# Attention's projections made for all batches in its first steps, experts dealt evenly over the steps, and the last batch divided on the chip

## The chip, the cores and the metric

The kernel runs on one core of one Trainium2 chip. The metric is the device time of the whole program in microseconds (us). The chip's engines are TensorE (PE in the profile; PEld is its weight load), VectorE (DVE), ScalarE (ACT), GpSimd (POOL) and SyncE (SP), which here only issues transfers. Each engine takes its instructions in order.

## What is computed

Eight batches of 512 tokens of width 256 pass through two layers, all in float32. Layer 0 is a state-space mixer and a mixture of experts; it is not changed here except for one small call. Layer 1, in the reference's own words cut short:

```python
xn = _layernorm(x)
q = x @ Wq;  latent_kv = (x @ Wk + x @ Wv) @ W_down_kv        # 256 -> 64
k_rec = latent_kv @ W_up_k;  v_rec = latent_kv @ W_up_v       # 64 -> 256
scores = clip(einsum('bhqd,bhkd->bhqk', qh, kh) * scale) * decay
out = softmax(clip(scores)) @ vh                               # 16 heads of 16
x = x + out @ Wo + ffn(xn)
```

The `ffn` sends each token to its two likeliest of eight experts; the eighth does nothing, and the other seven take at most 512 tokens each: `relu(in @ W1) @ W2`, scaled by the router's share and added to the token's row.

## The kernel before

**Layer 0** and the norm of layer 1 come first (up to about 1101 us). A generator `late` (line 576) makes the normed rows, keeps their transpose in HBM (`xtd1`), and makes batch 0's projections by calling `project`.

**The attention stage** starts at line 1281 with pools of its own; its schedule is written by hand from line 1486. There are 128 steps, `n` = 0 to 127: for each batch `b` (16 steps), each group `g` of four heads, each block `c` of 128 queries. In program order, round `n` of the loop issues:

- step n's scores (lines 1411 to 1422): four matmuls into `s_ps`, then on VectorE a clip, a multiplication by the decay band with a row maximum, and a negation;
- step n-1's four exponentials on ScalarE (line 1426);
- step n-2's transposes into `p_ps` (line 1433), four of 128 columns per head, and ScalarE's copies to `pT` (line 1434);
- in even rounds the product with v for two finished steps (`o_ps`, line 1442). I call a step even or odd by whether its round has that product.

Between these lie *slots*: calls of `fill` (line 1505), four a round up to round 63, then four in even rounds and three in odd ones. A slot takes one *piece* of other work, the first there is: the piece half done, then the list `urgent`, then `idle`. A piece is what a generator does up to its next `yield`. The other work:

- **Projections** (`project`, line 236, called through `inputs_of`, line 1294). For each batch: the latent (`lp`, 2 chains' worth of matmuls over 512 columns, copied to `lat` as 64 x 512), q (`qp`), k (`kp`), v (`vp`, four times 288 columns, with a row of ones in `lat` that makes the column of ones for the softmax sums). That is nine pieces. q and k pass through one buffer `qkc`, are stored in HBM (`qd`, `kd`) and loaded again by 32 transfers of 16 rows each that put each head on a 32-partition strip (`spread`, line 1274; six are issued each round by `load_some`). The pieces for batch b+1 enter `urgent` at round 16b + 6; its transposed input `xT` is asked at round 16b + 3.
- **Routing, sends, experts.** `follow` (line 1522) runs once a round: the rest of `late` in rounds 0 to 2, routing, then two `sends` a round (each scatters a tile of 128 rows to two slots by indirect transfers of GpSimd, line 1315, and has VectorE scale the tile into `x_sb`, line 1322). When these end, the round is called `ready` (25 here), and three rounds later `experts` (line 1221) enters `idle`. An expert's half is 17 pieces: one of transposes (`e_tp`), eight of the first layer (`e_hp`), eight of the second (`e_yp`, a quarter of a chain each). Fourteen halves are 238 pieces. Results are added to `x1` in HBM by GpSimd (line 1267).
- **Division and output.** After a group's last block `divide` (line 1448) copies `o_ps` to `os`, stores it in HBM (`od`), and for each pair of groups loads the heads back packed (`oT`, line 1466) and the sums by themselves (`sm`, line 1467), takes the reciprocals, sends them through HBM to be spread over partitions (`rb`), and multiplies (line 1478). Each of these steps is one round apart. Then `finish` (line 1371), four pieces in `urgent`, multiplies by Wo (`fin`) and adds into `x_sb`.
- **Combine** (line 1388): when no piece is left, `more` makes GpSimd add the eight batches of `x1` into `x_sb` by transfers (line 1391) and send out finished batches (line 1386); later batches go out as they finish.
- **The last batch's last two groups** are divided on the chip (`Ending`, line 1337): transpose, divide, transpose back, project, store. Groups 0 and 1 go through `divide` as in other batches.

`bank` is one PSUM buffer for all pieces of the stage, so that a piece's matmuls wait for the copy of the piece before.

Of the kernel before, what the change touches and what calls it, by code (L numbers as in the profile page):

```python
# [9 lines left out]
FP = mybir.dt.float32  # L10
# [7 lines left out]
P = 128  # L18
# [41 lines left out]
def tile_kernel(ctx: ExitStack, tc: tile.TileContext, t, out: bass.AP):  # L60
# [175 lines left out]
    def project(xT, lat, flat, vt, rows, bank, spread=None):  # L236


        lp = bank("lp", [DL, S])
        for k in range(KC):  # L240
            T.matmul(lp, w_kv[:, k, :], xT[:, k, :], start=(k == 0), stop=(k == KC - 1))  # L241
        A.copy(lat[:DL, :], lp)
        yield
        for n in ("q", "k"):
            fl = flat(n)
            for o in range(KC):
                ps = bank(n + "p", [P, S])
                if n == "q":
                    for k in range(KC):
                        T.matmul(  # L250
                            ps, w_q[:, k, o * P : (o + 1) * P], xT[:, k, :], start=(k == 0), stop=(k == KC - 1)
                        )
                    A.mul(fl[:, o, :], ps, 1.0 / 16.0)
                else:
                    T.matmul(ps, w_uk[:, o * P : (o + 1) * P], lat[:DL, :], start=True, stop=True)
                    A.copy(fl[:, o, :], ps)
                yield
            Y.dma_start(out=rows[n].rearrange("(o p) s -> p o s", p=P), in_=fl)
            if spread:
                spread(n)  # L260
        for c in range(TPB):
            vp = bank("vp", [P, VW])
            T.matmul(vp, lat[:, c * P : (c + 1) * P], w_uv, start=True, stop=True)  # L263
            A.copy(vt[:, c, :], vp)
            yield

    def rows_qk():
        return {n: dram.tile([DM, S], FP, name=n + "d", tag=n + "d", bufs=2) for n in ("q", "k")}
# [221 lines left out]
    with ExitStack() as es:  # L490
# [85 lines left out]
        def late():  # L576
# [19 lines left out]
            for b in range(B):  # L596
# [55 lines left out]
                if b == 0:  # L652
                    lat = tl.tile([DL + 1, S], FP, name="lat", tag="lat")
                    G.memset(lat[DL : DL + 1, :], 1.0)
                    yield from project(
                        xT, lat, lambda n: tl.tile([P, KC, S], FP, name=n + "c", tag="xn"), vt0, qk0,
                        lambda name, shape: bank(name, shape, "e"),
                    )

        def second_weights():  # L660

            nonlocal l1c, tl, w_r, rb, w_q, w_o, w_uk, w_uv, w_kv, band, slot1, iota_n, proj1, vt0, qk0
            es.close()
            l1c = ctx.enter_context(tc.tile_pool(name="l1c", bufs=1, side="right"))
            tl = tls.enter_context(tc.tile_pool(name="tl", bufs=1, side="right"))
            w_r = load("w_r", [P, KC, NE], l1c)
            rb = load("rb", [P, NE], l1c)
            w_q = load("w_q", [P, KC, DM], l1c)
            w_o = load("w_o", [P, KC, DM], l1c)
            w_uk = load("w_uk", [DL, DM], l1c)  # L670

            w_uv = ctile("w_uv", [DL + 1, VW], pool=l1c)
            G.memset(w_uv, 0.0)
            hv = w_uv[:, : AH * (AD + 1)].rearrange("p (h e) -> p h e", e=AD + 1)
            Y.dma_start(out=hv[:DL, :, :AD], in_=t["w_uv"])
            G.memset(hv[DL : DL + 1, :, AD : AD + 1], 1.0)
            slot1 = ctile("slot1", [P, NTILE, 2], I32, l1c)
            iota_n = ctile("iota_n", [P, NTILE], pool=l1c)
            G.iota(iota_n, pattern=[[P, NTILE]], base=-NT, channel_multiplier=1, allow_small_or_imprecise_dtypes=True)
            proj1 = ctile("proj1", [P, NTILE, NE], pool=l1c)  # L680
            vt0 = ctile("vt0", [P, TPB, VW], pool=l1c)
            qk0 = rows_qk()

            band = ctile("band", [P, NBAND], pool=l1c)
            G.iota(
                band, pattern=[[1, NBAND]], base=P - S, channel_multiplier=-1, allow_small_or_imprecise_dtypes=True
            )

            w_kv = ctile("w_kv", [P, KC, DL], pool=l1c)
            both = tl.tile([P, 2, KC, DM], FP, name="w_kt", tag="xr", bufs=2)  # L690
            Y.dma_start(out=both[:, 0], in_=t["w_kt"])
            Y.dma_start(out=both[:, 1], in_=t["w_vt"])
            w_dn = ctile("w_dn", [P, KC, DL], pool=tl)
            Y.dma_start(out=w_dn, in_=t["w_dn"])
            yield
            A.activation(band, band, AF.Abs)
            A.activation(band, band, AF.Exp, scale=-DECAY)
            V.tensor_tensor(both[:, 0], both[:, 0], both[:, 1], ALU.add)
            yield
            wp = bank("wp", [P, KC, DL], "e")  # L700
            for k in range(KC):
                for o in range(KC):
                    T.matmul(
                        wp[:, k, :], both[:, 0, o, k * P : (k + 1) * P], w_dn[:, o, :],
                        start=(o == 0), stop=(o == KC - 1),
                    )
            V.tensor_copy(w_kv, wp)
            yield
# [439 lines left out]
    with tc.tile_pool(name="a1", bufs=1) as p1, tc.tile_pool(name="a2", bufs=2) as p2, tc.tile_pool(  # L1148
# [125 lines left out]
        def spread(rows, got, n, by=None):  # L1274

            for g in range(4):
                wide = p2.tile([P, S], FP, name=n + "T", tag=n + "T", bufs=6)
                for i in range(4):
                    h = 4 * g + i
                    to, of = wide[32 * i : 32 * i + AD, :], rows[n][h * AD : (h + 1) * AD, :]  # L1280
# [4 lines left out]
                got[n].append(wide)  # L1285
# [8 lines left out]
        def inputs_of(b, xT, got):  # L1294
            rows = rows_qk()
            got["v"] = p2.tile([P, TPB, VW], FP, name="vt", tag="vt")
            yield from project(
                xT, lat, lambda n: p1.tile([P, KC, S], FP, name=n + "c", tag="qkc"), got["v"], rows, bank,
                lambda n: spread(rows, got, n),
            )  # L1300
# [26 lines left out]
        def ask_rows(b):  # L1327
            to_send[b] = r1b.tile([P, TPB, DW], FP, name="xs", tag="xs", bufs=B)
            Y.dma_start(out=to_send[b][:, :, :DM], in_=rows_of(xn1, b))
# [6 lines left out]

        class Ending:
# [3 lines left out]
            def __init__(self, b, c, op, held):  # L1341
                self.i, self.c, self.op, (self.oT, self.os) = b * TPB + c, c, op, held
# [6 lines left out]
            def divide(self):  # L1349
# [3 lines left out]
                tq = tq.rearrange("p g (i r) -> p (g i) r", r=32)  # L1353
                sm = p2.tile([P, 8], FP, name="smq", tag="smq")
                V.reciprocal(sm, tq[:, :, AD])
                self.oq = p2.tile([P, 8, AD], FP, name="oq", tag="oq")
                V.tensor_tensor(self.oq, tq[:, :, :AD], bc(sm, 2, [P, 8, AD]), ALU.mult)

            def back(self):
                tp = psum.tile([P, P], FP, name="tb", tag="s_ps", bufs=4)  # L1360
                T.transpose(tp, self.oq.rearrange("p h d -> p (h d)"), ident)
# [9 lines left out]
        def finish(b, oT):  # L1371
# [10 lines left out]
            if b in combined:  # L1382
                send(b)

        def send(b):
            G.dma_start(out=rows_of(out, b), in_=x_sb[:, b * TPB : (b + 1) * TPB, :])

        def combine():

            for b in range(B):  # L1390
                G.dma_start(out=x_sb[:, b * TPB : (b + 1) * TPB, :], in_=rows_of(x1, b), accum_op=ALU.add)
                combined.add(b)
            yield
            for b in finished:
                send(b)
# [52 lines left out]
        def divide(b, g, op, od, rd, held):  # L1448


            os = p1.tile([P, S], FP, name="os", tag="row", bufs=2)
            A.copy(os, op)
            if b == B - 1 and g == 2:
                held.append(os)
                return
# [27 lines left out]
        lat = p1.tile([DL + 1, S], FP, name="lat", tag="lat")  # L1483
        G.memset(lat[DL : DL + 1, :], 1.0)

        with tc.manual_schedule(engines=ENGINES):
            got = {"q": [], "k": [], "v": vt0}
            spread(qk0, got, "q", Y)
            spread(qk0, got, "k", A)
            finished, combined = set(), set()  # L1490
            urgent, idle, chains = [], [], []
# [3 lines left out]
            half_done = []  # L1495
            late_left = True
# [8 lines left out]
            def fill():  # L1505

                while queue := half_done or urgent or idle:
                    try:
                        if next(queue[0]):
# [8 lines left out]
            def more():  # L1518
                if ready is not None and n > ready + 3:
                    next(rows, None)  # L1520
# [23 lines left out]
            inputs = {0: got}  # L1544
            for n in range(N + 3):

                if n < N:
                    b, g, c = steps[n]
                    if (g, c) == (0, 3) and b + 1 < B:
                        xT = p2.tile([P, KC, S], FP, name="xT", tag="xT")  # L1550
                        Y.dma_start(out=xT, in_=xtd1[b + 1])
                    if (g, c) == (1, 2) and b + 1 < B:
                        inputs[b + 1] = {"q": [], "k": []}
                        urgent.append(inputs_of(b + 1, xT, inputs[b + 1]))
                    if (g, c) == (0, 0):
                        od = dram.tile([4, 4, 32, S], FP, name="od", tag="od", bufs=2)
                        rd = dram.tile([AH, S], FP, name="rd", tag="rd", bufs=2)
                        scratch = (od, rd, [])
                    now = Step(b, g, c, inputs[b])
# [3 lines left out]
                load_some(6)  # L1563
                if n == N + 1:
# [66 lines left out]
def layout(i):  # L1631
# [9 lines left out]
    def every(v):  # L1641
# [32 lines left out]
        "w_uv": i["L1_attn_W_up_v"].reshape(DL, AH, AD),  # L1674
# [28 lines left out]
```

## Time and profile before

| | |
|---|---|
| median of 3 runs | 2100.85 us (2100.71 to 2111.31) |
| the profiled execution | 2100.49 us; its span 2098.8 us, mean granted TensorE clock 0.933 |
| busy in the span | TensorE 1857.0 (88%), VectorE 1433.7 (68%), ScalarE 1178.8 (56%), GpSimd 629.1 (30%) |
| attention's first scores, first clip | 1103.98, 1106.09 us |
| first and last expert result sent (L1267) | 1366.9, 1975.3 us |
| mean of one exponential (L1426), one copy to pT (L1434), one clip (L1416) | 726, 590, 683 ns |

In the profile's groups a row gives line, engine, operation, output and inputs, shape and count; then busy time in us and the mean of one in ns; then the engine's idle time just before these instructions and what ended it. Busy times of neighbouring TensorE groups overlap, since matmuls are pipelined. A window's row gives its length, each engine's busy time and instruction count, the granted TensorE clock, the share of the DMA engines and the rate in GB/s.

### The profile page before, as it was taken

What the parts mean: (1) busy time and instruction counts of PE and PEld (TensorE: products, weight loads), DVE (VectorE), ACT (ScalarE), POOL (GpSimd) and SP (SyncE); (2) the same over time, 40 slices, a digit from 0 to 9 for tenths busy, and PEclk for the clock granted to TensorE, in tenths of its full rate; (3) what the DMA queues carried; (4) which work ended last, traced back from release to release, by engine and by line L of the source; (5) the groups of instructions that cost most, each with busy time, mean ns of one, the idle gap of its engine ahead of it and who ended that gap; (6) DMA issues with size and microseconds to landing.
All of it is one profiled execution on the core that took longest, in us unless ns stands there. A gap on an engine that the chain in (4) does not pass through costs nothing. (4 is left out here: it accounts for less than half of the span.)

```text
span 2098.8 us, 33158 instructions
## 1 busy us (share of the span) xinstructions
PE 1857.0 (88%) x11684; PEld 1227.0 (58%) x11684; DVE 1433.7 (68%) x3305; ACT 1178.8 (56%) x2548; POOL 629.1 (30%) x572
## 2 busy tenths in 40 slices
PE   5666999999999999977767877999999999999987
PEld 5333676677677677744544444566656666565544
DVE  5684757666575766678648976766666677777786
ACT  2243454535454454545425565767777777777776
POOL 0048645445464544445420154010000100000300
PEclk9877999999999999998876879899999999999989
DMA  7113654656564555444432232222312222221440
GB/s 260 61 51 113 224 192 161 202 175 201 166 205 152 195 184 174 140 145 133 148 100 96 80 115 69 78 82 64 88 53 83 67 85 85 64 89 52 74 129 27
DMA packets 150063, 255.03 MB, mean 122 GB/s; under 512 B 23457, under 2 KB 108116, under 8 KB 137992
## 3 DMA queue, kind: packets, MB, share of 16 engines
q1 hardware_dynamic: 111912, 132.31, 19.9%
q0 software_dynamic: 28512, 110.92, 17.0%
q10 hardware_dynamic: 9472, 9.67, 1.4%
q8 instruction: 93, 1.52, 0.3%
q14 instruction: 74, 0.61, 0.1%
HBM read 184.74 MB, written 73.09 MB: 123 GB/s over the span
## 5 line engine op out<-in xcount | busy, mean ns | idle before, releaser
L1416 DVE TENSOR_SCALAR s<-s_ps 128x512 f32<-128x512 f32 x512 | 317.7, 683 | 235.9 <-PE s_ps L1411 182.5
L1426 ACT ACTIVATE s<-s,ng 128x512 f32<-128x512 f32 x512 | 354.1, 726 | 24.1 <-DVE ng L1422 20.8
L1433 PE MATMUL p_ps<-ident,s 128*128 128x128 f32 x2048 | 296.8, 289 | 57.8 <-ACT pT L1434 49.8
L1433 PEld LDWEIGHTS p_ps<-ident,s 128*128 128x128 f32 x2048 | 245.3, 148 | 141.5 <-ACT pT L1434 84.8
L1418 DVE CUSTOM_DVE_ANT_0 s<-s,band 128x512 f32<-128x512 f32 x512 | 322.9, 687 | 0.0
L1434 ACT COPY pT<-p_ps 128x512 f32<-128x512 f32 x512 | 278.0, 590 | 72.1 <-PE p_ps L1433 57.1
L1267 POOL DMA_INDIRECT x<-e_yo,e_to x28 | 44.1, 1576 | 606.0 <-ACT e_yo L1266 541.0
L732 PE MATMUL pj<-xT,w_in 128*128 128x512 f32 x384 | 203.2, 656 | 16.6 <-DVE cv L745 13.7
L1411 PE MATMUL s_ps<-kT,qT 16*128 16x512 f32 x1024 | 167.3, 685 | 19.1 <-DVE s L1416 12.4
L544 PEld LDWEIGHTS h_ps<-xdT,w 128*128 128x128 f32 x1248 | 149.2, 192 | 22.4 <-issue 21.6
L544 PE MATMUL h_ps<-xdT,w 128*128 128x128 f32 x1248 | 152.8, 276 | 3.0 <-DMA w<-in_w_dram,w_idx 3.0
L745 DVE SCALAR_TENSOR_TENSOR cv<-pj,w_conv_w,cv 128x511 f32<-128x511 f32 (+2 forms) x192 | 143.1, 746 | 11.1 <-ACT cv L741 7.1
L562 PE MATMUL y_ps<-w,hT 128*128 128x256 f32 x624 | 148.9, 383 | 0.0
L908 POOL TENSOR_TENSOR au<-da,half 128x512 f32<-128x512 f32 x64 | 78.9, 1233 | 224.8 <-PE seg L924 122.7
L1442 PE MATMUL o_ps<-pT,vt 128*32 128x256 f32 x2048 | 139.4, 414 | 0.0
L562 PEld LDWEIGHTS y_ps<-w,hT 128*128 128x128 f32 x624 | 117.2, 193 | 32.5 <-issue 17.9
L732 PEld LDWEIGHTS pj<-xT,w_in 128*128 128x128 f32 x384 | 71.7, 205 | 100.0 <-issue 91.3
L982 POOL TENSOR_TENSOR yT<-yT,ex 128x512 f32<-128x512 f32 (+1 forms) x48 | 59.6, 1243 | 222.8 <-DVE ex L981 164.0
L1248 PE MATMUL e_hp<-e_xdT,e_w 128*128 128x256 f32 x448 | 121.7, 394 | 3.1 <-ACT e_xdT L1233 2.3
L1261 PE MATMUL e_yp<-e_w,e_hT 128*128 128x256 f32 x448 | 120.0, 390 | 0.2
L937 ACT ACTIVATE mt<-seg,mid 64x64 f32<-64x64 f32 x512 | 109.5, 309 | 0.8
L1442 PEld LDWEIGHTS o_ps<-pT,vt 128*32 128x32 f32 x2048 | 64.4, 117 | 77.9 <-issue 48.0
(292 smaller groups left out, 3019.6 us busy)
## 6 DMA issues: line engine op xcount, KB each, us to landing
ex<-exd SPq DMA_DIRECT2D x96, 128.0 KB
u<-in_u_dram SPq DMA_DIRECT2D x16, 512.0 KB
xtd<-xT SPq DMA_DIRECT2D x16, 512.0 KB
fr<-fdd SPq DMA_DIRECT2D x64, 128.0 KB
xT<-xtd SPq DMA_DIRECT2D x15, 512.0 KB
od<-os SPq DMA_DIRECT2D x30, 256.0 KB
e_w<-in_ei_dram SPq DMA_DIRECT2D x7, 1024.0 KB
e_w<-in_eo_dram SPq DMA_DIRECT2D x7, 1024.0 KB
```

What stands on the lines that cost most here:

```text
L544: T.matmul(hp[:, i, :], w1[:, k * FF + f * P : k * FF + (f + 1) * P], xdT[:, k * P : (k + 1) * P], start=(k == 0), stop=(k == KC - 1),)
L562: T.matmul(yp, hT[f // 4][:, f % 4, :], w2[:, f * DM : (f + 1) * DM], start=(f == 0), stop=(f == FC - 1))
L732: T.matmul(pj, w_in[:, k, o * P : (o + 1) * P], self.xT[:, k, :], start=(k == 0), stop=(k == KC - 1))
L745: V.scalar_tensor_tensor(cv[:, s:], pj[:, : S - s], conv_w[:, q, 3 - s : 4 - s], cv[:, s:], ALU.mult, ALU.add)
L1248: T.matmul(hp, w1[:, k, f * P : (f + 1) * P], xdT[:, k, :], start=(k == 0), stop=(k == KC - 1))
L1411: T.matmul(sp[i], self.q[r, cols], self.k[r, :], start=True, stop=True)
L1416: V.tensor_scalar(self.p[i], sp[i], -CLAMP, CLAMP, ALU.max, ALU.min)
L1418: V.tensor_tensor_reduce(out=self.p[i], in0=self.p[i], in1=band[:, at : at + S], scale=1.0, scalar=-3.0e38, op0=ALU.mult, op1=ALU.max, acc ...
L1426: A.activation(self.p[i], self.p[i], AF.Exp, bias=self.ng[:, i : i + 1])
L1433: T.transpose(pp[:, k, :], self.p[i][:, k * P : (k + 1) * P], ident)
L1434: A.copy(pT[i][:, :, cc * P : (cc + 1) * P], pp)
L1442: T.matmul(op[32 * i : 32 * i + 32, half * 2 * P : (half + 1) * 2 * P], self.v[:, k, h * (AD + 1) : h * (AD + 1) + 32], pT[i][:, k, :], st ...
```

## The change

1. `project` now lays the latent out in two halves: tokens 0 to 255 on partitions 0 to 63, 256 to 511 on 64 to 127. `lp` is four matmul calls of 256 columns instead of two of 512, and its copy is 128 x 256. k and v are made for each half from its own 64 partitions, with the up-projection weights present in both halves. v is made without the column of ones, in two copies instead of four; the ones are set once in the buffer. Seven pieces instead of nine.
2. `inputs`, a new generator, makes the projections of batches 1 to 7 one after the other, through two `qkc` buffers, stores q, k and v in HBM with room for all batches, and asks `xT` one batch ahead (for the first and the last batch at the batch's own start). Two of its pieces may be taken in each round once `late` has ended (`early`), before expert pieces and after urgent ones. `inputs_of(b + 1)`, at round 16b + 8, only loads v and lists the 32 loads of q and k.
3. Expert pieces are taken only while `spent < due()`: 238 pieces in equal shares over the rounds from `ready + 3` to 117.
4. The combine starts when all 238 are spent: batches 7 and 0 to 5 are added, batch 6 once it is finished, and then batches 0 to 6 are sent out together.
5. Batch 7's groups 0 and 1 are divided on the chip too (`first_heads`, eight pieces in `urgent`), each group copied to a buffer `ol`.
6. Four buffers instead of eight for the rows to be sent (`xs`). In layer 0's part two idle yields follow batch 0's projection, which has two pieces fewer.

```diff
+        lp = bank("lp", [P, HS])
         for k in range(KC):
-            T.matmul(lp, w_kv[:, k, :], xT[:, k, :], start=(k == 0), stop=(k == KC - 1))
-        A.copy(lat[:DL, :], lp)
+            for i, r in SIDES:
+                T.matmul(
+                    lp[r, :], w_kv[:, k, :], xT[:, k, i * HS : (i + 1) * HS], start=(k == 0), stop=(k == KC - 1)
+                )
+        A.copy(lat, lp)
...
+        for i, r in SIDES:
+            ps = bank("kp", [P, KC, HS])
             for o in range(KC):
+                T.matmul(ps[:, o, :], w_uk[r, o * P : (o + 1) * P], lat[r, :], start=True, stop=True)
+            A.copy(fl[:, :, i * HS : (i + 1) * HS], ps)
+            yield
...
+        for i, r in SIDES:
+            vp = bank("vp", [P, 2, AH * AD])
+            for c in range(2):
+                T.matmul(vp[:, c, :], lat[r, c * P : (c + 1) * P], w_uv[r, :], start=True, stop=True)
+            A.copy(
+                vt[:, 2 * i : 2 * i + 2, : AH * (AD + 1)].rearrange("p t (h e) -> p t h e", e=AD + 1)[:, :, :, :AD],
+                vp.rearrange("p t (h e) -> p t h e", e=AD),
+            )
+            yield
...
+        def inputs():
+
+            xT = {}
+
+            def ask_xT(b):
+                if b < B:
+                    xT[b] = p2.tile([P, KC, S], FP, name="xT", tag="xT")
+                    Y.dma_start(out=xT[b], in_=xtd1[b])
+
+            ask_xT(1)
+            for b in range(1, B):
+                if b + 1 < B - 1:
+                    ask_xT(b + 1)
+                elif b == B - 1:
+                    ask_xT(b)
+                    yield
+                rows = rows_qk()
+                yield from project(
+                    xT.pop(b), lat, lambda n: p1.tile([P, KC, S], FP, name=n + "c", tag="qkc", bufs=2), vt1, rows, bank
+                )
+                vd = dram.tile([P, TPB, VW], FP, name="vd", tag="vd", bufs=B)
+                Y.dma_start(out=vd, in_=vt1)
+                kept[b] = (rows, vd)
...
+        def first_heads(oT, os):
+
+            for c in range(TPB):
+                at = slice(c * P, (c + 1) * P)
+                tq = bank("tq", [P, 2, P])
+                for k in range(2):
+                    T.transpose(tq[:, k, :], os[k][:, at], ident)
+                oq = columns(tq)
+                yield
+                tp = bank("tb", [P, P])
+                T.transpose(tp, oq, ident)
+                A.copy(oT[:, 0, at], tp)
+                yield
...
+            for b in (B - 1, *range(B - 2)):
+                add(b)
+            yield
+            while B - 2 not in finished:
+                yield
+            add(B - 2)
+            for b in range(B - 1):
+                G.dma_start(out=rows_of(out, b), in_=x_sb[:, b * TPB : (b + 1) * TPB, :])
...
+            WORK = NE1 * 2 * (1 + FC + 2 * FC // 2)
+            LAST = 117
+            spent = 0
+
+            def due():
+
+                return WORK * (n - ready - 2) / (LAST - ready - 2)
...
-                while queue := half_done or urgent or idle:
+                nonlocal spent, early
+                while queue := half_done or urgent or (early and ahead) or (idle if idle and spent < due() else []):
                     try:
+                        early -= queue is ahead
+                        spent += queue[0] is work
...
             def more():
-                if ready is not None and n > ready + 3:
+                if spent == WORK:
                     next(rows, None)
...
                 load_some(6)
+                early = 0 if late_left else 2
```

## The prediction

> **What bounds the kernel now.** I read the slices first, then the chain that ended last, then windows of the trace cut where the attention stage changes character, then the groups and waits inside those windows.
>
> ```profile
> PE   5666999999999999977767877999999999999987
> ...
> PEclk9877999999999999998876879899999999999989
> ...
> PE 34%; ACT 7%; DVE 4%; DMA 2%; issue 2%; another core or an unknown queue 0%; ACTq 0%; DVEq 0%; SPq 0%
> ```
>
> A slice is 52.5 us. The change lives in the attention stage, slices 22 to 40 (from 1101 us). TensorE fills slices 26 to 38, and the chain is mostly TensorE. In slices 22 to 25 TensorE is not full (7, 8, 7, 7) and its clock is 0.6 to 0.9; the last two slices are not full either.
>
> ```profile
> core 0: us, PE busy (x) PEld busy (x) DVE busy (x) ACT busy (x) POOL busy (x), PEclk, DMA share, GB/s
> ...
> 1131.00:1181.00 50.00, 45.20 (x299) 26.71 (x297) 43.88 (x121) 36.74 (x67) 0.16 (x1) 0.87 0.22 75
> 1181.00:1337.00 156.00, 123.37 (x792) 68.06 (x796) 115.23 (x346) 91.17 (x163) 62.77 (x64) 0.78 0.28 89
> 1337.00:1664.00 327.00, 312.32 (x2250) 206.50 (x2243) 221.03 (x585) 236.27 (x452) 22.77 (x15) 1.00 0.25 71
> 1664.00:1978.00 314.00, 303.25 (x2226) 197.51 (x2225) 226.33 (x594) 235.87 (x453) 21.36 (x14) 0.99 0.26 74
> 1978.00:2021.00 43.00, 34.58 (x272) 19.12 (x274) 35.52 (x93) 32.37 (x58) 15.01 (x14) 0.89 0.88 193
> 2021.00:2099.00 78.00, 63.15 (x532) 38.96 (x524) 56.75 (x150) 56.52 (x107) 0.75 (x1) 0.95 0.09 29
> ```
>
> I place the 128 steps by each step's first clip (L1416). **Early**, steps 3 to 27 (1131 to 1337): routing and sends, loose, cold clock. **Middle**, steps 28 to 110 (1337 to 1978): experts, TensorE 96% busy. Steps 111 to 117 (1978 to 2021): experts gone, VectorE sets the pace, about 5.05 us an undisturbed step. **Tail**, 118 to the end: 78 us.
>
> ```profile
> L1433 PE MATMUL p_ps<-ident,s 128*128 128x128 f32 x1440 | 195.1, 277 | 23.4 <-ACT pT L1434 23.4
> L1248 PE MATMUL e_hp<-e_xdT,e_w 128*128 128x256 f32 x448 | 121.7, 394 | 3.1 <-ACT e_xdT L1233 2.3
> L1261 PE MATMUL e_yp<-e_w,e_hT 128*128 128x256 f32 x448 | 120.0, 390 | 0.2
> L1411 PE MATMUL s_ps<-kT,qT 16*128 16x512 f32 x720 | 106.3, 648 | 2.0 <-DVE s L1416 2.0
> L1442 PE MATMUL o_ps<-pT,vt 128*32 128x256 f32 x1432 | 88.9, 389 | 0.0
> L1375 PE MATMUL fin<-w_w_o,oT 128*128 128x256 f32 x80 | 22.7, 408 | 4.9 <-ACT kc L256 4.6
> L250 PE MATMUL qp<-xT,w_w_q 128*128 128x512 f32 x40 | 19.6, 613 | 0.0
> L263 PE MATMUL vp<-w_uv,lat 65*128 65x288 f32 x40 | 13.7, 424 | 0.0
> L255 PE MATMUL kp<-lat,w_w_uk 64*128 64x512 f32 x20 | 11.2, 641 | 0.0
> L241 PE MATMUL lp<-xT,w_kv 128*64 128x512 f32 x20 | 9.7, 605 | 0.0
> ```
>
> ScalarE's groups of the same window have this row:
>
> ```profile
> L256 ACT COPY kc<-kp 128x512 f32<-128x512 f32 x10 | 5.9, 586 | 11.9 <-PE kp L255 6.6 <-DMA qd<-qc 5.2
> ```
>
> The first fence has TensorE's groups of 1337 to 2021, 90 steps. A step's own TensorE work is (195.1 + 106.3 + 88.9) / 90 = 4.33 us. Five batches' projections, qp + vp + kp + lp, add 54.2 us, 10.84 each; five finishes 22.7. The L256 row shows the single projection buffer at work: k's copy waited 5.2 us for q's store. And after 1980:
>
> ```profile
> DVE sm L1472 <- DMA sm<-od: 4.1, 1, 4.1
> ```
>
> VectorE, the pace setter there, stands 4.1 us behind the tiny load of batch 6's sums, at 2015.7, just after the combine's burst (DMA share 0.88 in that window).
>
> **Part by part: the projections leave the middle.** Groups overlap: with e_tp's 8.8 us they sum to 717.7, against 650.1 us of busy TensorE (the three windows' sum). So 54.2 us is 54.2 x 0.906 = 49 of busy time; at 96% busy, 51 us. Steps 37 to 41, with a projection and a finish, took 42.4 us; their other work (5 x 4.33, seven expert pieces at 0.86, four finish pieces at 1.13) explains 32, leaving 10. The two agree: **-51 us**. The q-store wait goes too; it lies inside these 51, as SPq's loads do.
>
> **Experts dealt evenly.** 238 pieces over steps 28 to 117 are 2.64 a step. Steps 64 to 69 hold neither projection nor finish: 44.0 us and 21 pieces, so a piece costs (44.0 - 6 x 4.33) / 21 = 0.86 us. Steps 111 to 117 give 43 - 7 x 4.33 = 13 us of TensorE slack. A dealt step then needs 4.33 + 2.64 x 0.86 = 6.6 us, above VectorE's 5.05 (5.7 with its divisions) and ScalarE's 5.4 (504.5 busy in that window, less the projections' 23, over 90): TensorE sets it. **-13 us**. In the other direction, odd steps (no values) with three pieces waited 0.43 us for ScalarE (6.31 us, 5.88 busy), so I give back **+2**, with bounds 0 and +25 (0.3 us a step). Together 684 becomes 622.
>
> **Seven projections in steps 3 to 28.** 50 pieces at two a step; four slots exist before step 64, urgent work first, so they fit, and batch 1 is complete (8 calls, steps 3 to 6) before step 8 asks for it. Per batch: lp was two chains of 512 columns, 1.93 us; two column halves may run side by side, as the four 32-wide strips of L1442 do (32 matmuls in 1.93 us in the timeline), so 0.97 to 1.93. [...] The old lp, kp and vp rows already had 64 columns or 64 rows, and their price of 10 us was measured in place[...]. [...] by the L1442 row it halves. I take 0.97; the difference, 7 us in all, goes into the range. kp and vp: 16 matmuls of 256 columns at finish's 1.13 us per four are 4.5, qp 3.9. Sum 9.4, x 0.906 = 8.5 us; seven are 60, and 20 were there: **+40 us of TensorE work at full clock**.
>
> How much shows? At full clock the early work is 25 x 4.33 + 20 + 4.5 + 1.3 = 134 us of its 206. After the change 174. What stays: seven TensorE gaps of 2 us and more during the sends, 23 us (the largest have ScalarE waiting on an unknown queue); 3 us for batch 1's xT, now asked in the very piece that reads it (a 512 KB transfer took 2.8), with scores and transposes queued behind it on TensorE; about 12 for cold windows after stalls; 4% ordinary idle, 7; 3 where routing holds VectorE. Total 222, **+16 us**. Two readings bound it. [...] The row says 0.78 in the sends, but 1131 to 1181, with a projection inside, 0.87. If the clock stays at 0.78, 40 / 0.78 = 51 us shows in full: early 257. If the work only fills idle time: 206, or 200 with a warmer base. I take 222 because the 0.87 row, denser, is the nearer.
>
> **Side costs.** SPq: the stores of q and k and the xT loads move among the sends' xs loads and the first divisions' loads; a store waits for ScalarE's copy, a us or so, and what queues behind it is asked steps ahead. The store and reload of v are 14 more issues at about 0.4 us, over 100 steps. All k and q loads start at a batch's step 8 with six a step; done by 14. I cost all this at nothing; without that slack a late kT would cost its 2 to 3 us. xs with four buffers: a load waits for scatters issued two steps, some 15 us, earlier: 0, at most a few us on SPq. Weights and memsets of v before 1101: 0, bounds -3 to +3. ScalarE: v in two copies instead of four: inside the sum.
>
> **Last batch and combine.** Batch 7's groups 0 and 1: four times two transposes, a reciprocal (0.20) and a multiply (0.29), a transpose, a 0.27 copy: about 2.0 us of VectorE, against 0.35 x 2 + 0.69 x 2 before: +1, where VectorE sets the pace. No loads of sums behind the burst: the 4.1 us was batch 6's and goes because the burst now starts after step 117; it is inside the 13. The burst (some 27 us from 1979.5) moves into steps 118 to 126, where nothing loads. ScalarE's 3 us disturbances move with it: +3. The expert generator's end raises the counter past its target, so what remains of the write-back is issued after the loop; GpSimd has nothing else queued, so its place costs nothing. It waits for batch 6's finish (about 60 us before the end) and needs about 30. Tail 78 + 4 = 82.
>
> Sum on the profiled execution (2100.49, span 2098.8 and 1.7 around it): 2100.5 - 51 - 13 + 2 + 16 + 4 = **2058.5 us**. The median is 2100.85, nearly the same; I say 2058.
>
> **Rivals.** *Pieces at full cold price*: early 257, total 2094. For it: projections around 1290 cost about their full price. Against: those stood four to a step behind a 3 us store wait. *All hidden*: early 200, tail 80: 2034; for it, 206 us with 134 of work. *Slower: the dealt middle loses the clock.* Steps 111 to 117, 80% busy, ran at 0.89. If 90 steps of thinner work did so, 601 / 0.89 / 0.96 = 703 us instead of 622: 2140. It decides below a mean clock of about 0.94. Against it: a dealt step needs 6.6 us of TensorE where the next engine needs 5.7, about what gave 1.00. *It does not do what it says*, experts still bunched: 13 us back, 2072.
>
> **Chances.** Forecast with its sizes (2040 to 2078, bunching in it) 0.62; all hidden 0.18; cold price 0.13; lost clock or worse 0.07. Range 2028 to 2094. About 0.5%, 10.5 us, is what a measurement can tell from no change: faster 0.83, within 0.11, slower 0.06.
>
> **What would show it.** Clock 0.85 or more between steps 3 and 28 and that stretch near 222 us; experts' rows equal in every slice to step 117, with TensorE 95% busy and 6.9 us a step (right), or gaps on ScalarE's pT (wrong); no kc wait on qd, no sm wait; two or three lp pieces of 1 us. I am wrong above all if the early stretch passes 250 us or the middle's clock leaves 1.0.

## The result, and the profile after

The changed kernel takes **2071.68 us**, median of 4 runs (2069.31 to 2077.54). The kernel before took 2105.11 us on the same chip (4 runs). The ratio is 0.9843 with a 95% interval of 0.9805 to 0.9882: faster by 33 us. The profiled execution took 2070.49 us (span 2068.8) against 2100.49 us (span 2098.8) before: 30 us less. The forecast of 2058 was 13.7 us too low; its range held the time.

Every ratio below is against the kernel before on the same chip, because chips differ: beside the experiments it took 2104, 2103.5, 2093 and 2066 us. Stretches of steps are compared between traces of different chips too; the chips differed in the early steps (last section), while the same code's steps 28 to 117 took 674.5 us on one and 672.7 on another.

The slices and the chain of the page after, in the same order as before:

```profile
PE   5676999999999999987776998899999999999987
...
PEclk9877999999999999999776999899999999999999
...
PE 36%; ACT 7%; DVE 4%; issue 1%; another core or an unknown queue 1%; DMA 1%; ACTq 0%; SPq 0%; DVEq 0%
```

A slice is now 51.7 us. In slices 23 to 25 TensorE was 8, 7, 7 and is 9, 9, 8, and the clock was 8, 7, 9 and is 9, 9, 9; slice 26, 9 before, is 8. The loose stretch has filled up. The windows show it better. They are cut where the stages begin, as in the prediction:

```profile
core 0: us, PE busy (x) PEld busy (x) DVE busy (x) ACT busy (x) POOL busy (x), PEclk, DMA share, GB/s
...
1130.00:1187.00 57.00, 53.70 (x328) 29.41 (x326) 43.66 (x120) 35.17 (x66) 0.14 (x1) 0.88 0.34 119
1187.00:1351.00 164.00, 142.97 (x904) 80.28 (x903) 115.44 (x346) 104.82 (x191) 63.16 (x65) 0.89 0.42 139
1351.00:1367.00 16.00, 14.57 (x106) 9.01 (x107) 11.35 (x32) 12.84 (x24) 0.00 (x0) 1.00 0.55 163
1367.00:1665.00 298.00, 284.27 (x2192) 190.80 (x2194) 227.33 (x594) 228.80 (x433) 20.17 (x13) 1.00 0.25 71
1665.00:1982.00 317.00, 303.14 (x2364) 206.19 (x2360) 244.09 (x645) 245.36 (x466) 23.28 (x15) 0.99 0.23 64
1982.00:2005.00 23.00, 20.89 (x184) 12.75 (x188) 21.90 (x55) 20.12 (x38) 14.18 (x13) 1.00 1.08 168
2005.00:2033.00 28.00, 20.88 (x144) 12.69 (x136) 17.26 (x50) 15.27 (x30) 1.51 (x2) 0.76 0.43 145
2033.00:2069.00 36.00, 26.28 (x224) 16.65 (x220) 18.52 (x51) 22.69 (x46) 0.00 (x0) 1.00 0.05 16
```

In the sends (1187 to 1351) TensorE is 87% busy where it was 79%, and its clock 0.89 where it was 0.78. The middle (1367 to 1982) is 95 and 96% busy at a clock of 1.00 and 0.99. And a new weak place has appeared: in 2005 to 2033 every engine is under 75% busy and the clock falls to 0.76.

Put on the steps, each begun by its first clip in the two traces (us):

| stretch | before | after | difference | forecast |
|---|---|---|---|---|
| up to the first clip | 1106.1 | 1104.4 | -1.7 | 0 |
| steps 0 to 2 | 24.5 | 25.4 | +0.9 | 0 |
| early, 3 to 27 | 206.1 | 221.2 | +15.1 | +16 |
| middle, 28 to 117 | 684.3 | 631.0 | -53.3 | -62 |
| 118 to 121 | 25.1 | 23.2 | -1.9 | |
| 122 to 124 | 15.4 | 27.9 | +12.5 | |
| 125 to the end | 37.3 | 35.6 | -1.7 | |
| tail, 118 to the end | 77.8 | 86.7 | +8.9 | +4 |

### The profile page after: what moved, and what is told of

Read it like the earlier page. It is cut to its first block, busy times and chain, and to the rows that moved or that the text cites. A ratio compares the mean times of both kernels' runs of the same rounds, so it can differ in the third digit from the quotient of the medians.

```text
span 2068.8 us, 33318 instructions
## 1 busy us (share of the span) xinstructions
PE 1840.4 (89%) x11760; PEld 1229.3 (59%) x11760; DVE 1436.3 (69%) x3311; ACT 1174.8 (57%) x2536; POOL 628.1 (30%) x572
## 4 chain that ended last, share of the span: by engine, by line
PE 36%; ACT 7%; DVE 4%; issue 1%; another core or an unknown queue 1%; DMA 1%; ACTq 0%; SPq 0%; DVEq 0%
PE p_ps L1493 8%; PE s_ps L1471 6%; PE o_ps L1502 6%; PE e_yp L1275 5%; PE e_hp L1262 5%; ACT s L1486 3%; ACT pT L1494 2%; PE qp L254 1%; DVE s L1478 1%; DVE s L1476 1%; PE fin L1434 1%; PE vp L269 1%; PE kp L262 1%; PE op L896 0%
## 5 line engine op out<-in xcount | busy, mean ns | idle before, releaser
L1493 PE MATMUL p_ps<-ident,s 128*128 128x128 f32 x2048 | 288.6, 284 | 53.9 <-ACT pT L1494 48.9
L1493 PEld LDWEIGHTS p_ps<-ident,s 128*128 128x128 f32 x2048 | 239.0, 144 | 119.8 <-ACT pT L1494 77.5
L1502 PE MATMUL o_ps<-pT,vt 128*32 128x256 f32 x2048 | 134.0, 396 | 2.0 <-issue 1.8
L763 ACT ACTIVATE th<-cv 128x512 f32<-128x512 f32 x64 | 40.3, 630 | 117.0 <-DVE cv L759 113.2
```

The costliest lines, as they stand in the source:

```text
L1493: T.transpose(pp[:, k, :], self.p[i][:, k * P : (k + 1) * P], ident)
L1502: T.matmul(op[32 * i : 32 * i + 32, half * 2 * P : (half + 1) * 2 * P], self.v[:, k, h * (AD + 1) : h * (AD + 1) + 32], pT[i][:, k, :], st ...
```

## The theories

**Theory.** TensorE sets the middle (95 and 96% busy there), so work taken out of it, or spread over steps that had room, comes off the time. Moved to the early steps, about half of the same work fills idle time or is paid for by a faster clock there (0.89 in the sends instead of 0.78). The tail lost because TensorE, taking instructions in order, stands behind the small divisions of batch 7's first groups on VectorE (6.6 us in three waits from 1982 to 2033). **Rivals.** (a) The projections' place matters little; the gain is that of the second `qkc` buffer, which ends k's wait for q's store. (b) The even deal does it alone. (c) The tail's loss comes from the combine's burst, which now lies there, and not from the divisions.

## Taking parts of the change back

**The even deal.** Experts taken as soon as there is a slot, with the rest of the change kept.

```diff
-... or (idle if idle and spent < due() else []):
+... or (idle if idle and spent < WORK else []):
```

> Changed kernel, but expert pieces are taken as soon as a slot is free, as before the change. If dealing evenly is what fills the loose steps (my step: 13 us less 2): experts end about step 97, some 20 steps then run at VectorE's 5.05 us with about 0.7 us of idle TensorE each, and the total is 2080 (2076 to 2085). If the even deal bunches pieces so much that it gains nothing: 2072, within 4 us of the changed kernel.

Measured: 2088.1 us, ratio 0.9927 (0.9908 to 0.9946). Against the changed kernel's 0.9843 that is about 18 us. In the trace the middle took 646.1 us instead of 631.0: the experts ended at step 96, and the undisturbed steps after it took 5.04 us each, VectorE's pace. The deal is worth 15 to 18 us here, where I expected 8, and nearly half of the gain is there without it. Rival (b) is out.

**The last batch by HBM.** Groups 0 and 1 of batch 7 go through `divide` again.

```diff
-            if b == B - 1:
-                ...first_heads, both groups held in SBUF...
-                return
+            if b == B - 1 and g == 2:
+                held.append(os)
+                return
```

> Changed kernel, but groups 0 and 1 of the last batch are divided through HBM as before. If the 13 us that steps 122 to 124 take above 5.05 each come from the heads' pieces (TensorE standing behind VectorE's small divisions): about 2062. If they come from the write-back burst that now lies there, the loads of the division wait in it as well: 2072 to 2080.

Measured: 2060.97 us, ratio 0.9794 (0.9749 to 0.9838). Steps 122 to 124 took 16.5 us instead of 27.9, and everything else stayed (early 218.8, middle 632.3, 125 to the end 36.3). The burst is still in its new place, so rival (c) is out: the divisions on the chip cost 11 us. The windows of these three steps, in the changed kernel and then here:

```profile
2005.30:2033.18 27.88, 20.76 (x141) 12.64 (x134) 16.99 (x48) 15.40 (x30) 1.51 (x2) 0.76 0.41 143
2009.42:2025.88 16.46, 13.80 (x136) 8.27 (x128) 15.38 (x41) 15.34 (x27) 1.51 (x2) 1.00 0.84 285
```

TensorE is idle for 7.1 us instead of 2.7, and busy for 20.8 us at a clock of 0.76 instead of 13.8 at 1.00. By these rows some 4.5 of the 11.4 us are waits, about 5 the lower clock (20.76 x 0.24, an estimate), and about 2 added work.

**Their place.** The eight pieces one a round, as other divisions go, instead of in all slots of three rounds.

```diff
-urgent.insert(0, first_heads(held[0], held[1:]))
+chains.append(first_heads(held[0], held[1:]))
```

> Changed kernel; the last batch's first groups are still divided on the chip, but one piece a round (taken where the division chains are), so that a transpose back comes a round after its division. If what cost 11 us was TensorE standing behind VectorE's small divisions in the same round: about 2060, as with the division through HBM. If the division on the chip costs by itself (VectorE's added work where it sets the pace): 2068 or more.

Measured: 2065.8 us, ratio 0.9832 (0.9790 to 0.9873), hardly apart from the changed kernel. Half right: steps 122 to 124 fell to 16.5 us, but the eight rounds then ran into the end, and 125 to the end took 43.2 us instead of 35.6. Spreading took the wait away where VectorE is full (19.0 us busy of the 20 from 2005), and put some of it where nothing hides it (+7.6 us).

**One buffer for q and k.** Everything else is kept.

```diff
-..., tag="qkc", bufs=2)
+..., tag="qkc", bufs=1)
```

> Changed kernel with one qkc buffer instead of two. If k's copy then stands about 2.8 us behind q's store seven times, with ScalarE's other work queued behind it: the early stretch is 10 to 20 us longer, 2082 to 2092. If two pieces a round already stand far enough apart for the store to land: 2072.

Measured: 2100.73 us, ratio 0.9989 (0.9971 to 1.0007): nearly the whole gain is gone, where I expected 10 to 20 us. The waits from 1130 to 1390 us, the early steps and steps 28 and 29 (engine, line and tile, what it waited for: us in all, times, longest):

```profile
ACT kc L263 <- DMA qd<-qc: 24.5, 4, 11.5
...
PE kp L262 <- ACT kc L263: 10.1, 1, 10.1
```

and the timeline of the longest of them (start, us, engine, line, operation; in brackets the idle time before it and what ended it):

```profile
1362.93 0.60 ACT L255 ACTIVATE qc<-qp 128x512 f32<-128x512 f32 x1
...
1369.97 0.35 DVE L1537 RECIPROCAL sm<-sm 128x32 f32<-128x32 f32 x1
1370.35 0.34 SPq L1538 DMA_DIRECT2D rd<-sm  x1
1371.77 0.60 SPq L1540 DMA_DIRECT2D rb<-rd  x1
1372.48 0.40 SPq L257 DMA_DIRECT2D qd<-qc  x1
1377.20 0.58 ACT L263 COPY kc<-kp 128x512 f32<-128x512 f32 x1 [11.47 <-DMA qd<-qc]
1377.84 2.07 PE L262 MATMUL kp<-lat,w_uk 64*128 64x256 f32 x4 [10.07 <-ACT kc L263]
```

q is ready at 1363.5, but SyncE's queue issues its store at 1372.48. Ahead of it in that queue stands the store of a division's reciprocals (L1538), and that waits for VectorE, which reaches the reciprocal at 1369.97 behind a step's clips. Then ScalarE stands at k's copy with all its later exponentials and copies behind it, and TensorE stands too. Of ScalarE's 11.5 us, 6.8 pass before the store is issued and 4.7 after it. One small reciprocal on one engine more than doubled the wait of two others, through a queue that only issues. The second longest of the four waits, 10.3 us, also ends with a store that was issued behind a division's reciprocals (1218.70, then 1220.83); the other two are 2.0 and 0.7 us. The second buffer doesn't make the store earlier (in the changed kernel the last q is ready at 1349.6 and its store is issued at 1358.6, again behind a division's reciprocals at 1356.5); it lets nobody wait for it.

**The second buffer alone**, in the kernel before.

```diff
-..., tag="qkc")
+..., tag="qkc", bufs=2)
```

> The kernel before with two qkc buffers and nothing else. Its k copies waited 8.1 us for q's stores in all seven batches (2.9 in the early stretch, 5.2 later). If the second buffer is worth what the rows show: 6 to 10 us less, 2096 at a before of 2104. If it is worth the 29 us that one buffer costs in the changed kernel: 2075.

Measured: 2084.67 us against 2093.38, ratio 0.9939 (0.9921 to 0.9958): -13 us by the ratio, -9 by the medians, about what the rows promised. So rival (a) holds for less than half of the 33 us: 9 to 13 in the old place. In the new place the same buffer is worth some 30 us; 21.8 us of its 24.5 us of waits are the two behind the reciprocals' stores.

**No projections at all** for batches 1 to 7.

```diff
 def inputs():
-    ...the seven batches' projections...
+    for b in range(1, B):
+        kept[b] = (qk0, vd)
+    yield
```

> Changed kernel without the projections of batches 1 to 7; all batches use batch 0's q, k and v, so this part of the computation is left out. It prices the 60 us of projection work where it now lies. My prediction's working (early stretch 222 us, of which idle time hid part) gives an early stretch of about 185 to 195 and 2035 to 2045. All hidden: 2065 or more. Full price at a cold clock: 2000 or less.

Measured: 2045.8 us, ratio 0.9725 (0.9677 to 0.9773). The early stretch took 196.0 us instead of 221.2, the middle 624.1 instead of 631.0 (5.2 of these 7 us are in steps 28 to 30: the last projection's k and v are made in steps 28 and 29, and one expert piece moves on to step 30). So 60 us of TensorE work at full clock (the prediction's sum for seven projections) cost 32 us in these two stretches, and 25 to 27 us in the whole, since this run's first step began later and its tail was 3 us longer. Time and early stretch are just above what I expected. Steps 3 to 27 without the projections, and then with them in the changed kernel:

```profile
1131.80:1327.85 196.05, 159.46 (x1033) 93.51 (x1036) 158.65 (x466) 121.17 (x211) 63.13 (x65) 0.74 0.26 84
1129.80:1351.03 221.23, 196.90 (x1229) 109.92 (x1230) 159.31 (x465) 140.22 (x255) 63.30 (x65) 0.88 0.40 134
```

TensorE was busy 159.5 us at a granted clock of 0.74, against 196.9 us at 0.88 with the projections. Busy time times clock, an estimate of the work at full clock, gives 118 and 173 us. Of these 55 us more work, 25 show as time; 12 filled idle time (36.6 to 24.3 us), and 18, by the same estimate, are what the faster clock gave back (busy time above work, 41 to 24 us). The denser stretch had the faster clock.

**One projection piece a round** from round 8 on, instead of two.

```diff
-early = 0 if late_left else 2
+early = 0 if late_left else 2 if n < 8 else 1
```

> Changed kernel; from round 8 one projection piece a round instead of two, so that about half of the projections lie in the rounds of the experts. Leaving them out gained 25 us of the early stretch for 60 us of TensorE work; where TensorE is 96% busy they pay in full. So half of them moved: early stretch some 12 shorter, middle some 30 longer, about 2088. If two pieces a round overload the early stretch and one a round hides: 2060.

Measured: 2093.93 us, ratio 0.9949 (0.9922 to 0.9975). Early 207.7 us (-13.5), steps 28 to 110 613.0 (+28.2). Each us saved in the early steps costs two in the middle. Both kernels have the second buffer, so this is the run that shows, against rival (a), that the projections' place counts.

## Putting parts into the kernel before

**The even deal alone**, without the new combine order.

```diff
-while queue := half_done or urgent or idle:
+while queue := half_done or urgent or (idle if idle and spent < due() else []):
...
-if ready is not None and n > ready + 3:
+if spent == WORK:
     next(rows, None)
```

> The kernel before with the experts dealt evenly to step 117 and the combine after it; projections, buffers and the last batch's division as before. My step gave 13 us less 2. In the changed kernel the greedy order cost 16. If the deal works by itself: 2090 to 2094 at a before of 2104. If it pays only once projections no longer fill whole rounds: within 5 us of before. If the loads of batch 6's and 7's divisions stand in the later burst: 5 to 10 us of it lost again.

Measured: 2103.22 us against 2093.38, ratio 1.0046 (1.0030 to 1.0063): slower. The step that I had costed came as costed: steps 28 to 117 took 674.5 us instead of 684.3, -9.8 (forecast -13 + 2 = -11). But step 119 took 22.56 us. The waits after 1980 us:

```profile
PEld fin L1375 <- ACT fo L1377: 17.0, 1, 17.0
ACT fo L1377 <- DVE x_sb L1379: 16.5, 1, 16.5
PE fin L1375 <- ACT fo L1377: 16.2, 1, 16.2
DVE x_sb L1379 <- DMA x_sb<-x: 16.1, 1, 16.1
```

Read from the bottom: VectorE adds batch 6's output into `x_sb` and waits 16.1 us for GpSimd's combine transfer into the same rows; ScalarE's next copy waits for VectorE, and TensorE for ScalarE. The deal moves the combine's start behind the last expert, onto batch 6's finish.

**The deal with the changed kernel's combine** (batch 7 and 0 to 5 first, 6 once finished).

```diff
 if spent == WORK:
     next(rows, None)
...
-    ...combine as before...
+    for b in (B - 1, *range(B - 2)):
+        add(b)
+    yield
+    while B - 2 not in finished:
+        yield
+    add(B - 2)
```

> As e10, with the changed kernel's combine: batch 6 is added to x_sb only once it is finished, and batches 0 to 6 go out together after that. In e10 steps 118 to 121 took 42 us instead of 25, with VectorE's add of batch 6's finish 16.1 us behind the combine's transfer into the same rows, while the middle was 10 us shorter. If that wait is all that made e10 slower: no such wait, steps 118 to 121 about 25, and about 10 us under before (ratio 0.995, against e10's 1.0046). If the later burst slows these steps by itself: the ratio stays above 1.

Measured: 2059.27 us against 2065.98, ratio 0.9963 (0.9944 to 0.9983), -7.6 us: a little less than expected, and the sign has turned. Steps 118 to 121 took 23.2 us instead of 42.1, with no such wait. What I had costed at nothing is what lets the even deal pay at all.

## Going further

**A strict deal.** In the changed kernel the piece half done goes on past its share; here it doesn't.

```diff
-while queue := half_done or urgent or (early and ahead) or (idle if ...):
+while queue := (half_done if half_done and (urgent or spent < due()) else []) or (
+    [] if half_done else urgent or (early and ahead) or (idle if ...)):
```

> Changed kernel; a half-done chain of the second expert layer no longer goes on past its share, so no round takes more than its 2.64 pieces. In the changed kernel an even step with four pieces took 8.54 us and the odd step after it, with one, 5.0 to 5.6 with TensorE idle up to 1.4; three and two take 7.6 and 5.45. If this bunching is where the middle lost its 9 us: middle 8 to 12 shorter, 2061. If not: 2072.

Measured: 2060.79 us, ratio 0.9799 (0.9759 to 0.9838); steps 28 to 110 took 572.8 us instead of 584.8. Steps 84 and 85 of the changed kernel, an even one with four pieces and an odd one with one:

```profile
1746.32:1754.85 8.53, 8.53 (x73) 5.77 (x74) 5.36 (x14) 5.09 (x9) 1.55 (x1) 1.00 0.17 21
1754.85:1760.39 5.54, 4.16 (x29) 2.77 (x30) 5.10 (x14) 4.53 (x9) 1.55 (x1) 1.00 0.34 71
```

and the same two with the strict deal, two and three pieces:

```profile
1738.09:1745.45 7.36, 7.07 (x65) 4.37 (x66) 5.36 (x14) 4.63 (x9) 1.55 (x1) 1.00 0.19 25
1745.45:1751.07 5.62, 5.62 (x37) 4.17 (x38) 5.10 (x14) 5.30 (x10) 0.38 (x1) 1.00 0.14 47
```

TensorE is busy 12.69 us over both steps in both kernels. In the first the odd step is too thin, the pace is VectorE's (5.10 us busy of 5.54) and 1.38 us of TensorE lie idle; in the second 0.29 us. Of the 44 even steps from 30 to 117, 17 take four pieces in the changed kernel and 5 with the strict deal.

**Even steps given less**, since they hold the product with v.

```diff
-return WORK * (n - ready - 2) / (LAST - ready - 2)
+return WORK * (n - ready - 2) / (LAST - ready - 2) - (0.7 if n % 2 == 0 else 0)
```

> As e7, and even rounds, which have the product with v, are held back 0.7 of a piece, so that they take two and odd rounds three. By the changed kernel's own steps (even with two 6.4, odd with three 6.3) a pair is 12.7 for five pieces against 13.1 to 13.8: middle 15 to 25 shorter than the changed kernel's, 2050. If odd steps with three wait more on ScalarE: 2061 or more.

Measured: 2070.55 us, ratio 0.9855 (0.9806 to 0.9903): a miss, it lost the gain of the strict deal (steps 28 to 110: 583.7 us). The step that failed: I took 6.4 us for an even step with two pieces. The row just shown is 7.36 us with two, and with three such steps take 7.67 (median): taking a piece out of an even step saves only 0.3 us. The pair as a whole, from the steps without other work: even with two and odd with three took 13.35 us (mean of 13 pairs in this run), even with three and odd with two 12.84 (mean of 6 in the strict deal's).

**Strict deal and last batch by HBM together.**

> Changed kernel with the last batch's first groups divided through HBM as before (e2) and the strict deal (e7). The two act in different steps, so their 11 us each should add: 2050, steps 28 to 117 about 618 us and steps 122 to 124 about 16. If they share a cause: 2060.

Measured: 2049.49 us against 2093.38, ratio 0.9780 (0.9741 to 0.9819). Both gains are there in its trace: steps 28 to 117 took 618.0 us, and 122 to 124 17.4. The time looks like the 2050 forecast, but this chip's kernel before is 10 us faster than the 2104 that I had reckoned from: by ratios, 0.978 stands for a forecast of 0.974. It is the fastest of the complete versions by its ratio, though its interval just overlaps the changed kernel's, and largely those of the two edits alone. Were the two edits' differences from the changed kernel simply added, the ratio would be 0.9843 - 0.0049 - 0.0044 = 0.9750, inside the interval.

## Why the prediction was nearly right

**The projections leave the middle (-51), the even deal (-13 + 2).** Together -53.3 instead of -62. The mechanism held: the clock stayed at 0.99 to 1.00 and TensorE 95% busy, so the rival that costs the clock didn't come. The term that was mis-sized is bunching: "+2, with bounds 0 and +25". I looked at odd steps with too many pieces; what came was even steps with four and odd steps with one, and the strict deal shows 12 us of it. Another 7 us are the projections' overrun into the middle, 5 of them in steps 28 to 30, where I had put the projections wholly early (the run without them: 624.1 against 631.0). That is 19 us of which I had allowed 2, so the rest of my middle was some 8 us too dear (631.0 - 19 = 612, where 622 - 2 = 620 was forecast). My rival "experts still bunched: 13 us back, 2072" thus names the right cause, within pairs of steps and not over whole slices; that its 2072 is the measured time is luck, since the tail is in that as well.

**Seven projections in the early steps (+16).** It was +15.1, and the clock 0.88 (I asked for 0.85 or more). The sum is right partly by luck: two of its parts were 12 us off, one up and one down. TensorE's work at full clock was some 173 us, as taken (174). But busy time lost to a clock below full took 24 us instead of 12 (196.9 - 173, by the estimate above), and idle time 24 instead of 36 (23 + 3 + 7 + 3); the 3 us for batch 1's xT didn't appear: it was asked at 1129.75 and used at 1136.42 with no idle time ahead of it. Matmuls of one later projection in TensorE's timeline:

```profile
1163.85 1.08 PE L245 MATMUL lp<-xT,w_kv 128*64 128x256 f32 x8
...
1183.10 1.13 PE L262 MATMUL kp<-lat,w_uk 64*128 64x256 f32 x4
```

Eight lp matmuls of 256 columns took 1.08 us where the two chains of 512 columns had taken 1.93: the halves ran side by side, in six of the seven batches at a granted clock of 1.00 (batch 1's took 1.97 us at 0.50). 1.08 is 0.11 above half of 1.93: the row of L1442, from which I had taken the halving, was the right guide. That nothing at all would be gained, the other end of my range, no trace had shown. kp is at the 1.13 that I had taken from fin.

**The q-store wait, "inside these 51".** A lump that hid a dependence: the second buffer is worth 9 to 13 us in the old place and some 30 in the new. Without it the whole change brings nothing that stands out (ratio 0.9989), so the sum came near only because the change holds that buffer: the forecast gave it no term. **The side costs "at nothing" on SPq** hold only because nobody waits there; the e3 rows show the store 9 us late in its queue. In the changed kernel there is no kc wait on qd, as asked.

**Last batch and combine (+4).** Tail +8.9. The step that failed: "about 2.0 us of VectorE, against 0.35 x 2 + 0.69 x 2 before: +1, where VectorE sets the pace". VectorE's 2 us are right; what I left out is who stands behind them. The waits of 1982 to 2033 in the changed kernel:

```profile
ACT oT L1397 <- PE tb L1396: 10.5, 4, 5.3
PEld tb L1396 <- issue: 9.0, 4, 2.7
...
PE tb L1396 <- DVE oq L1383: 6.6, 3, 2.5
```

and one of the four in the timeline:

```profile
2027.41 0.08 DVE L1478 DVE_READ_ACCUMULATOR2_ANT mx<- 128x1 f32 x1
2027.53 0.17 DVE L1482 TENSOR_SCALAR ng<-mx 128x4 f32<-128x4 f32 x1
2027.61 0.20 DVE L1381 RECIPROCAL smq<-tq 128x8 f32<-128x8 f32 x1
2027.85 0.29 DVE L1383 TENSOR_TENSOR oq<-tq,smq 128x128 f32<-128x128 f32 x1
...
2028.28 0.30 PE L1396 MATMUL tb<-ident,oq 128*128 128x128 f32 x1 [2.23 <-DVE oq L1383]
2028.62 0.27 ACT L1397 COPY oT<-tb 128x128 f32<-128x128 f32 x1 [5.31 <-PE tb L1396]
2033.18 2.48 DVE L1476 TENSOR_SCALAR s<-s_ps 128x512 f32<-128x512 f32 x4 [5.05 <-PE s_ps L1471]
```

The 0.2 us reciprocal comes behind a whole step's clips and band multiplications. TensorE's transpose back waits for it, and in TensorE's order the next scores and transposes stand behind that transpose; so ScalarE idles 5.31 us and then VectorE itself 5.05. The lower clock, 0.76 over these steps, lengthens the work that then remains (about 5 us, the estimate from the run that divides through HBM). Steps 122 to 124 took 9.85, 7.42 and 10.62 us instead of about 5.05 each: +12.5. The rest of the tail was better than forecast: the burst's "+3" did not come (steps 118 to 121 and the end -1.9 and -1.7, and 122 to 124 only +1.1 in the run that divides through HBM), and the 4.1 us wait for sums is gone. By the forecast's steps the 12 us between 2058.5 and 2070.5 are -1.7 + 0.9 (start), -0.9 (early), +8.7 (middle) and +4.9 (tail).

## What to carry to other kernels

Price a small operation handed between engines by what is queued behind whoever waits for it, not by its own time: 2 us on VectorE cost 11 to 12, of which about 5, an estimate, through a TensorE clock of 0.76 instead of 1.00. Work moved into a stretch with idle time can cost half of its own time or less: here 25 to 32 us of 60, with a clock that rose from 0.74 to 0.88. But buffers that were enough in its old place have to be counted anew in the new one (the second one was worth 9 to 13 us, then some 30). When work is spread evenly, ask what else was ordered by its end (here the combine), and deal in units that let each step, not only the mean, stay above the pace of the next engine (12 us with the strict deal).

## What the runs showed of the hardware

- **Chips differ in the sends.** On the fastest chip (kernel before 2066 us) the kernel with the deal and the new combine, whose early steps are those of the kernel before, had an early stretch of 174.8 us, where the kernel with the deal alone had 199.9 on another. There ScalarE's copies waited 12.9 us in five waits and 3.8 in one for a queue that the profile doesn't know; on the fast chip no such wait is in this stretch. Whether these waits make the whole difference, and what they are, was not tried and stays open.
- **Adding TensorE work to the early steps raised their granted clock, but the busy share alone doesn't tell the clock.** It was 0.74 with TensorE 81% busy (159.5 of 196.0) and 0.88 at 89% (196.9 of 221.2); the middle had 1.00 at 95%. Yet two stretches of the changed kernel's tail, 75% busy (2005 to 2033) and 73% busy (2033 to 2069), had 0.76 and 1.00. In the first TensorE stood still three times for 1.8 to 2.5 us, up to 2011.0, 2020.9 and 2028.3, in the second never for more than 1.6. Soon after each of the three the clock read 0.50 (2012 to 2018, 2022 to 2025, 2029 to 2032) and between them 1.00 (2019 to 2021, 2026 to 2028). Yet in the kernel before TensorE stood still for 2.21 us up to 1240.32, and the clock was 1.00 from 1238 to 1246. What decides stays open.
- **Two column halves of one matmul ran side by side** in float32 between differently shaped neighbours: 1.08 us instead of 1.93 at a clock of 1.00, in six of seven batches.
